# A decoder's quantised cross attention takes in the MLP behind it, pair by pair

## The chip, the cores and the metric

The program runs on one core of a Trainium2 chip. Its metric is the device time of one execution in microseconds (us). The median of three timed runs of the kernel before is 2883.2 us (2880.36 to 2885.45).

The engines are called as the profile calls them: PE is TensorE's matmuls and PEld its weight loads, DVE is VectorE, ACT is ScalarE, POOL is GpSimd, SP is SyncE, whose queue issues most DMAs here.

## What is computed

The reference is a decoder of two layers on 2048 tokens (16 tiles of 128) with 256 features. Each layer is a self attention, a cross attention and an MLP, each with a residual and a layer norm behind it. The change touches the first layer's cross attention and MLP:

```python
x = _layernorm(x + xattn(x, ctx_2048))
x = _layernorm(x + ffn(x))

# xattn: 16 heads of 16 features, 2048 queries, 2048 keys
q = fq_sym((x @ Wq + bq) * 0.25)       # 8-bit steps, one scale for a row of a head
k = fq_sym(k); v = fq_sym(v)
attn = fq_unsigned(softmax(q @ k.T))   # 0..255, one scale for a row
out  = (attn @ v) @ Wp + bp

# ffn: 1024 hidden features
h   = silu(x @ Wg.T) * (x @ Wu.T)
out = h @ Wd.T
```

## The kernel before

**Cross attention.** Keys and values are quantised first. Then a loop runs over 128 steps, `(gp, i, u)`: eight pairs `gp` of token tiles, eight pairs `i` of heads, the two tiles `u` of the pair. A step makes the scores of one tile of 128 queries for two heads against all 2048 keys.

- `scores` (L719) is called four times a step, for each half of the keys and each of the two heads. Two bf16 matmuls (L725) fill a PSUM tile `s` of two banks (three such tiles exist); DVE scales it, writes it to `e` and takes its maximum (L726). The queries stand as three copies of 16 rows in 64 rows for each head, and the key tile holds both heads in its 128 rows. For one head the other 64 rows of `qz` are zero, so a matmul runs over all 128 rows.
- `exponent` (L736): DVE reduces the four maxima to two (L738), and ACT adds ln 255 (L740).
- `weights8` (L742): ACT takes the exponential to 8 bits and its row sum (L749), and a transposing DMA on SP's queue moves it (L757).
- `spread` (L760): POOL casts the transposed bytes to bf16 (L761).
- `context` (L766): PE multiplies with the values (L771), 16 matmuls for two steps, three to four steps after the scores, in the chunks of `turns` (L810).
- `sums`, `divide`, `output` (L779 to L805) finish the pair before: reciprocals of the row sums, spread out by DVE copies (L786) and transposed by PE, the product (L796), the output projection (L802) and the residual (L805). The projection's weights `wp` are scaled by the values' scale on DVE (L697) and then laid out as `wp4` by 16 DMAs (L702).
- The queries of the next pair are made meanwhile (`query_rows`, `query_cols`, L559 and L568): a projection, and DVE instructions L542 to L549 and L563, a POOL product (L550), PE transposes (L556) and ACT copies (L572).
- The layer norm is done for four tiles at a time, `norm` (L102 to L116) and `norm_T` (L119), in every second pair: statistics, then the reciprocal root by a logarithm and an exponential on ACT (L100, L101), then a tensor_scalar on DVE (L114).

**MLP.** It begins when the cross attention has ended (L875 to L913). Both weights are loaded (3 MB). For each of four groups of 512 tokens: eight times a gate and an up product (L891), silu on ACT (L894), the product on DVE (L895); then the down product (L905), the residual (L908), and the norm of the group before.

**What sets the order.** Inside both loops the order of PE's instructions is the order of the program text (`manual_schedule`); in the MLP that holds for ACT instead. The other engines' order is made by the scheduler of the language from costs and dependences. An engine runs its instructions in that order, each waiting for its own inputs and buffers. PSUM has eight banks: six for the three `s` tiles, one for `o` of the context, one, `misc`, for everything else in the loop.

Of the kernel before, what the change touches and what calls it, by code (L numbers as in the profile page):

```python
# [18 lines left out]
F32 = mybir.dt.float32  # L19
# [29 lines left out]
def decoder(ctx: ExitStack, tc: tile.TileContext, w: dict, out: bass.AP):  # L49
# [28 lines left out]
    nc.gpsimd.memset(eps5, 1e-5)  # L78
    eps6 = const.tile([P, 1], F32, name="eps6")
# [40 lines left out]
    def norm_T(g, k, psum, tag):  # L120

        pt = psum.tile([P, 4, P], F32, tag=tag, name="ln_pt")
        for i in range(4):
            nc.tensor.transpose(pt[:, i, :], xs[4 * g + i][:, k * P : (k + 1) * P], ident)
        nc.scalar.copy(xT[g][:, k, :], pt.rearrange("p a b -> p (a b)"))

# [396 lines left out]
    with ExitStack() as ph:  # L523
# [5 lines left out]
        rows3 = [pool.tile([P, 16, 64], BF16, name=f"rows3_{i}") for i in range(2)]  # L529

        qz = [pool.tile([P, 2, 8, P], BF16, name=f"qz{i}") for i in range(4)]

        def quantised(wk, lhsT, weights, bias, scale, psum, tag):
# [3 lines left out]
            for k in range(2):  # L537
                nc.tensor.matmul(
                    pq.rearrange("p h d -> p (h d)"), lhsT=lhsT(k), rhs=weights[:, k, :], start=k == 0, stop=k == 1
                )  # L540
            a = wk.tile([P, 16, 16], F32, tag="qa", name="qa", bufs=2)
            nc.vector.tensor_tensor(a, pq, bias.rearrange("p (h d) -> p h d", h=16), ALU.add)  # L542
            s = stat.tile([P, 16], F32, tag="qs", name="qs")
            nc.vector.tensor_reduce(s, a, AX.X, ALU.max, apply_absolute_value=True)
            nc.vector.tensor_scalar(s, s, scale / 127.0, 1e-8, ALU.mult, ALU.max)
            r = stat.tile([P, 16], F32, tag="qr", name="qr")
            nc.vector.reciprocal(r, s)
            if scale != 1.0:
                nc.vector.tensor_scalar_mul(r, r, scale)  # L549
            nc.gpsimd.tensor_tensor(a, a, bc(r, 2, 16), ALU.mult)  # L550
            return a, s

        def transposed3(rows, psum, tag):
            pt = psum.tile([P, 8, P], BF16, tag=tag, name="pt3")
            for i in range(8):
                nc.tensor.transpose(pt[:, i, :], rows[:, 2 * i : 2 * i + 2, :].rearrange("p h d -> p (h d)"), ident16)  # L556
            return pt

        def query_rows(t, wk, psum, tag):  # L559

            a, s = quantised(wk, lambda k: xTt(t, k), wq, bq, 0.25, psum, tag)
            rows = rows3[t % 2]
            nc.vector.tensor_scalar(  # L563
                rows[:, :, 0:48].rearrange("p h (r d) -> p h r d", r=3), bc(a, 2, 3), ROUND, ROUND, ALU.add, ALU.subtract
            )
            return rows, s

        def query_cols(t, rows, psum, tag):  # L568
            pt = transposed3(rows, psum, tag)
            for hh in range(2):  # L570
                half = slice(64 * hh, 64 * hh + 64)
                nc.scalar.copy(qz[t % 4][half, hh], pt[half])  # L572
            return qz[t % 4]

        qs = {}
        with tc.tile_pool(name="l0x_1", bufs=1) as p1, tc.tile_pool(name="l0x_p0", bufs=2, space=PSUM) as ps0:
# [9 lines left out]
            wp = load_w(pool, "L0_xattn_Wp")  # L586
# [84 lines left out]
            for n in range(NB + 4):  # L671
# [7 lines left out]
                if n == 3:  # L679
                    for t in rows3 + qz:  # L680
                        nc.vector.memset(t, 0.0)
                if n in (5, 7):
                    t = (n - 5) // 2
                    qs[t] = query_rows(t, p1, ps0, "pk")
                if n in (6, 8):
                    t = (n - 6) // 2
                    rows, sq = qs[t]
                    qs[t] = (query_cols(t, rows, ps0, "pt3"), sq)
# [7 lines left out]
        for c in range(2):  # L696
            nc.vector.tensor_scalar(wp[:, c], wp[:, c], sv[:, c : c + 1], None, ALU.mult)  # L697
        wp4 = pool.tile([P, 4, HID], F32, name="wp4")
        nc.gpsimd.memset(wp4, 0.0)
        for h in range(16):  # L700
            at = slice(16 * (h % 8), 16 * (h % 8) + 16)
            nc.sync.dma_start(out=wp4[at, 2 * (h // 8) + h % 2, :], in_=wp[at, h // 8, :])  # L702
        ln255 = pool.tile([P, 1], F32, name="ln255")
# [10 lines left out]
        def group(gp):  # L714
            ssum = stat.tile([P, 2, 16], F32, tag="ssum", name="ssum", bufs=3)
            ot = wk.tile([P, 2, 2, 2 * P], F32, tag="ot", name="ot")
            groups[gp] = (None, ssum, ot)

        def scores(gp, i, u, half, hh, st):  # L719

            qT, sq = qs[2 * gp + u]
# [693 lines left out]
```

## Time and profile before

| what | value |
|---|---|
| median of three runs | 2883.2 us |
| the profiled execution's own time | 2880.24 us |
| its span, first to last instruction | 2878.5 us |
| mean granted TensorE clock | 0.974 |
| PE busy | 2589.4 us (90%) |
| DVE busy | 1988.7 us (69%) |
| ACT busy | 1500.2 us (52%) |
| POOL busy | 1093.5 us (38%) |
| loop of the cross attention, first to last eviction | 884.0 to 1606.0 us |
| its end: last contexts, divides, outputs, norm | 1606.0 to 1637.0 us |
| MLP, up to the next layer's first matmul | 1637.0 to 1809.6 us |

Busy shares are means over stages with different limits: PE's 90% comes from the stages around the cross attention. Inside it the shares are to be read from windows of time. Idle time of an engine that isn't the bottleneck costs nothing. A line of a group gives its source line, engine, operation, what is written and read with partitions and elements, the count, the busy time and the mean duration of one in ns, and the idle time of the engine just before these instructions with what ended it.

### The profile page before, as it was taken

The page shows a single profiled execution, that of the slowest core. Times are in us where ns is not written, and L with a number is a line of the kernel's source. Part 1 is how long each engine was busy: PE and PEld are TensorE (multiplying, and loading weights), DVE is VectorE, ACT ScalarE, POOL GpSimd, SP SyncE. Part 2 cuts the span into 40 slices and gives each one's busy share as a digit, 9 for nine tenths or more (in the row PEclk, how much of TensorE's full clock was granted, in tenths as well). Part 3 has the DMA queues.
Part 4 walks back from the last instruction along what each step waited for, and adds up shares of the span by engine and source line. Part 5 has one row for each costly group of instructions (what it writes and reads, how often), then busy time and mean ns, then how long its engine had stood idle before and what let it go on. Part 6 is the DMA issues. An engine that isn't in the chain of part 4 may idle for free.

```text
span 2878.5 us, 38462 instructions
## 1 busy us (share of the span) xinstructions
PE 2589.4 (90%) x13790; PEld 1555.3 (54%) x13868; DVE 1988.7 (69%) x4688; ACT 1500.2 (52%) x2719; POOL 1093.5 (38%) x1070
## 2 busy tenths in 40 slices
PE   6999999999976877877778699999988899999998
PEld 3677777777752333333333365566655546565646
DVE  5677877777768999999999422677877753334231
ACT  3455555555536888888888412455545432213120
POOL 4644444444465666676667400522222200000000
PEclk9999999999998999999999899999999999999999
DMA  6000000000013554554545400200010000000000
GB/s 215 1 1 1 1 1 1 1 1 1 1 52 69 93 94 85 93 98 88 91 89 96 127 12 0 96 2 1 2 52 10 3 1 0 8 1 8 0 8 8
DMA packets 298734, 108.92 MB, mean 38 GB/s; under 512 B 273328, under 2 KB 291216, under 8 KB 297776
## 3 DMA queue, kind: packets, MB, share of 16 engines
q1 hardware_dynamic: 297152, 102.65, 16.3%
q0 software_dynamic: 1392, 3.81, 0.6%
q8 instruction: 109, 1.79, 0.3%
q14 instruction: 81, 0.66, 0.1%
HBM read 36.96 MB, written 2.10 MB: 14 GB/s over the span
## 4 chain that ended last, share of the span: by engine, by line
PE 63%; DVE 20%; ACT 7%; issue 5%; POOL 2%; DMA 2%; another core or an unknown queue 0%; SPq 0%; DVEq 0%; ACTq 0%; POOLq 0%
DVE e L726 13%; PE proj L310 11%; PE gate L1322 6%; PE py L1354 6%; PE up L1322 6%; ACT a L749 4%; PE po L437 4%; PE sc L1036 3%; PE tp L1056 3%; PE o L1066 2%; PE sc L356 2%; PE pm L427 2%; PE gate L891 2%; PE pm L426 2%; PE py L905 2%
## 5 line engine op out<-in xcount | busy, mean ns | idle before, releaser
L726 DVE TENSOR_SCALAR_CACHE_REDUCE e<-s,qs 128x1024 f32<-128x1024 f32 x512 | 630.7, 1273 | 14.1 <-DMA wp<-w_L_xattn_Wp 7.7
L761 POOL CAST aT<-at 128x2048 bf16<-128x2048 uint8 x256 | 485.6, 1901 | 246.7 <-DMA at<-a 233.8
L749 ACT ACTIVATE a<-e,snl 128x2048 uint8<-128x2048 f32 x256 | 511.1, 1997 | 4.9
L725 PE MATMUL s<-kT,qz 128*128 128x512 bf16 x1001 | 309.1, 395 | 125.6 <-DVE e L726 121.5
L771 PE MATMUL o<-aT,vq 128*128 128x512 bf16 x1000 | 295.5, 399 | 26.7 <-POOL aT L761 22.1
L725 PEld LDWEIGHTS <-qz 128*128 128x128 bf16 x1024 | 101.6, 100 | 288.8 <-issue 217.9
L1326 DVE TENSOR_TENSOR h<-h,up 128x512 f32<-128x512 f32 (+1 forms) x100 | 68.8, 688 | 194.7 <-PE up L1322 193.2
L771 PEld LDWEIGHTS <-vq 128*128 128x128 bf16 x1024 | 103.2, 101 | 164.1 <-issue 50.2
L1325 ACT ACTIVATE h<-gate 128x512 f32<-128x512 f32 (+1 forms) x100 | 59.8, 598 | 238.3 <-PE gate L1322 238.1
L1322 PE MATMUL gate<-xT,w_L_ffn_w1g 128*128 128x512 f32 x352 | 167.8, 596 | 0.0
L1322 PE MATMUL up<-xT,w_L_ffn_w1u 128*128 128x512 f32 x352 | 165.4, 592 | 0.0
L1045 DVE TENSOR_REDUCE amx<-sc 128x8 f32<-128x1024 f32 x96 | 116.7, 1215 | 56.9 <-PE sc L1036 56.7
L1354 PE MATMUL py<-w_L_ffn_w2T,h 128*128 128x256 f32 x704 | 154.6, 379 | 0.0
L1048 ACT ACTIVATE pr<-pr 128x1024 f32<-128x1024 f32 x96 | 101.6, 1059 | 89.1 <-DVE pr L1047 89.0
L1057 ACT COPY prT<-tp 128x512 f32<-128x512 f32 x192 | 104.1, 584 | 76.9 <-PE tp L1056 76.6
L1354 PEld LDWEIGHTS py<-w_L_ffn_w2T,h 128*128 128x128 f32 x704 | 133.7, 190 | 18.3
L380 ACT ACTIVATE pls<-sc,lm,rms_rs 128x128 f32<-128x128 f32 x256 | 113.8, 454 | 21.7 <-DVE lm L376 21.7
L310 PE MATMUL proj<-Wlk,xT 128*128 128x512 f32 x256 | 121.9, 599 | 2.9 <-ACT raw_Wlv L336 1.7
L310 PE MATMUL proj<-Wq,xT 128*128 128x512 f32 x256 | 122.4, 601 | 0.6 <-DVE raw_Wlk L319 0.6
L437 PE MATMUL po<-Wo,mT 128*128 128x256 f32 x512 | 121.2, 380 | 1.4 <-ACT mT L429 1.4
L310 PE MATMUL proj<-Wlv,xT 128*128 128x512 f32 x256 | 121.3, 596 | 0.0
L1047 DVE TENSOR_TENSOR pr<-sc,amx 128x1024 f32<-128x1024 f32 x96 | 117.0, 1219 | 5.7
(304 smaller groups left out, 5336.2 us busy)
## 6 DMA issues: line engine op xcount, KB each, us to landing
at<-a SPq DMA_TRANSPOSE x256
w_L_ffn_w1g<-in_L_ffn_w1g SPq DMA_DIRECT2D x1, 2816.0 KB
w_L_ffn_w1u<-in_L_ffn_w1u SPq DMA_DIRECT2D x1, 2816.0 KB
w_L_ffn_w2T<-in_L_ffn_w2T SPq DMA_DIRECT2D x1, 2816.0 KB
xT<-in_xT SPq DMA_DIRECT2D x4, 512.0 KB
Wlk<-in_L_attn_Wlk SPq DMA_DIRECT2D x4, 512.0 KB
Wq<-in_L_attn_Wq SPq DMA_DIRECT2D x4, 512.0 KB
Wlv<-in_L_attn_Wlv SPq DMA_DIRECT2D x4, 512.0 KB
```

What stands on the lines that cost most here:

```text
L310: nc.tensor.matmul(pp.rearrange("p h d -> p (h d)"), lhsT=xTt(b, k), rhs=wts[nm, hg][:, k, :], start=k == 0, stop=k == 1)
L380: nc.scalar.activation(pls[:, h, :], by_head[:, h // 2, h % 2, NC4:NK], AF.Exp, bias=nm[:, h : h + 1], scale=rq[:, h : h + 1], accum_out=s ...
L437: nc.tensor.matmul(outs[b], lhsT=st["mT"][:, h, :], rhs=wts["Wo", hg][:, h, :], start=hg == 0 and h == 0, stop=hg == 3 and h == 3,)
L725: nc.tensor.matmul(s[:, c, :], lhsT=qT[:, hh, i, :], rhs=kT[:, i, at : at + G], start=True, stop=True)
L726: nc.vector.tensor_scalar(st["e"][hh][:, half, :], s.rearrange("p a b -> p (a b)"), sq[:, 2 * i + hh : 2 * i + hh + 1], None, ALU.mult, AL ...
L749: nc.scalar.activation(a.bitcast(U8), st["e"][hh].rearrange("p a b -> p (a b)"), AF.Exp, bias=st["nm"][:, hh : hh + 1], accum_out=groups[g ...
L761: nc.gpsimd.tensor_copy(aT[:, :, hh, u * P : (u + 1) * P].rearrange("p (b j) q -> p b j q", j=2), st["at"][hh].bitcast(U8).rearrange("p b ...
L771: nc.tensor.matmul(o.rearrange("p a b -> p (a b)"), lhsT=vq[:, n, c * P : (c + 1) * P], rhs=aT[:, n].rearrange("p a b -> p (a b)"), start= ...
L1045: nc.vector.tensor_reduce(mx, sc, AX.X, ALU.max)
L1047: nc.vector.tensor_tensor(pr, sc, bc(mx, 2, P), ALU.subtract)
L1322: nc.tensor.matmul(pp[:rows], lhsT=wt[:, k, :], rhs=xT[g][:, k, :], start=k == 0, stop=k == 1)
L1354: nc.tensor.matmul(py, lhsT=h[:rows, i4 * P : (i4 + 1) * P], rhs=wt, start=n == 0, stop=n == len(parts) - 1)
```

## The change

The first layer's MLP becomes part of the cross attention's loop. While pair `gp` has its scores made, pair `gp - 1` goes through its norm and its gate and up products (256 tokens at a time), and pair `gp - 2` through its down product. Only the last pair's MLP stands behind the loop. In particular:

- The MLP's gate and up weights no longer fit beside the loop's buffers. They are loaded again for each pair in 128 KB pieces, three buffers ahead of PE; for the last pair they are loaded once, into a buffer of `aT`.
- silu(g) is written as 0.5 g (1 + tanh(g/2)). ACT takes the tanh and copies gate and up out of PSUM, DVE makes (tanh + 1) g, POOL multiplies with up, and the 0.5 goes into the residual.
- The layer norms of these stages are made for pairs (`norm_pair`): the reciprocal root by a power on POOL, the subtraction and product by a scalar_tensor_tensor.
- The two heads' scores are made by matmuls over 64 rows each, one head in each row half; `qz` with its zeros becomes `qT`. The matmuls of a half-step's two `s` tiles alternate.
- The maximum of the second half starts from that of the first, and `exponent` becomes one scalar_tensor_tensor on DVE with a tile of ln 255.
- Three small steps of the query quantising, the copies of the reciprocals and the scaling of `wp4` move from DVE to POOL. The buffers of `a` go from five to four.

```diff
+    def norm_pair(q):
+        mv = stat.tile([P, 2, 2], F32, tag="np_mv", name="np_mv")
+        for i in range(2):
+            st = stat.tile([P, 6], F32, tag="ln_st", name="ln_st")
+            nc.vector.bn_stats(out=st, in_=xs[2 * q + i])
+            nc.vector.bn_aggr(out=mv[:, i, :], in_=st)
+        rstd = stat.tile([P, 2], F32, tag="np_rstd", name="np_rstd")
+        nc.gpsimd.tensor_scalar(rstd, mv[:, :, 1], 1.0, 1e-5, ALU.mult, ALU.add)
+        nc.gpsimd.tensor_tensor(rstd, rstd, mhalf, ALU.pow)
+        for i in range(2):
+            x = xs[2 * q + i]
+            nc.vector.scalar_tensor_tensor(
+                x, x, mv[:, i, 0:1], rstd[:, i : i + 1].to_broadcast([P, HID]), ALU.subtract, ALU.mult
+            )
...
         def query_rows(t, wk, psum, tag):
...
-            nc.vector.tensor_scalar(s, s, scale / 127.0, 1e-8, ALU.mult, ALU.max)
+            nc.gpsimd.tensor_scalar(s, s, 0.25 / 127.0, 1e-8, ALU.mult, ALU.max)
             r = stat.tile([P, 16], F32, tag="qr", name="qr")
             nc.vector.reciprocal(r, s)
-            if scale != 1.0:
-                nc.vector.tensor_scalar_mul(r, r, scale)
             nc.gpsimd.tensor_tensor(a, a, bc(r, 2, 16), ALU.mult)
+            nc.gpsimd.tensor_scalar(a, a, 0.25, ROUND, ALU.mult, ALU.add)
+            nc.gpsimd.tensor_scalar(
+                rows3[:, :, 0:48].rearrange("p h (r d) -> p h r d", r=3), bc(a, 2, 3), 1.0, -ROUND, ALU.mult, ALU.add
+            )
...
+        def scores(gp, i, u, half, st):
+            t = 2 * gp + u
+            s = [ps.tile([P, 2, G], F32, tag="s", name="s", bufs=3) for _ in range(2)]
             for c in range(2):
                 at = (2 * half + c) * G
+                for hh in range(2):
+                    r = slice(64 * hh, 64 * hh + 64)
+                    nc.tensor.matmul(
+                        s[hh][:, c, :], lhsT=qT[t % 4][r, i, :], rhs=kT[r, i, at : at + G], start=True, stop=True
+                    )
+            for hh in range(2):
+                nc.vector.tensor_scalar(
+                    st["e"][hh][:, half, :],
+                    s[hh].rearrange("p a b -> p (a b)"),
+                    qs[t][:, 2 * i + hh : 2 * i + hh + 1],
+                    None if half == 0 else st["mx"][:, 0, hh : hh + 1],
+                    ALU.mult,
+                    ALU.max,
+                    accum_out=st["mx"][:, half, hh : hh + 1],
+                )
 
         def exponent(st):
-            nm = stat.tile([P, 2], F32, tag="snm", name="snm")
-            nc.vector.tensor_reduce(nm, st["mx"], AX.X, ALU.max, negate=True)
             st["nm"] = stat.tile([P, 2], F32, tag="snl", name="snl")
-            nc.scalar.activation(st["nm"], nm, AF.Identity, bias=ln255)
+            nc.vector.scalar_tensor_tensor(st["nm"], st["mx"][:, 1, :], -1.0, ln255, ALU.mult, ALU.add)
...
+        def ffn_load(j):
+            i, n = j // 2, j % 2
+            t = wgu[i, n] = wk.tile([P, 2, P], F32, tag="wgu", name="wgu", bufs=3)
+            nc.sync.dma_start(out=t, in_=gu_dram[n, i])
...
+        def ffn_gate(q, i, n, tag="misc"):
+            if n == 0:
+                pp = ps.tile([P, 2, G] if tag == "s" else [P, 2, 2 * P], F32, tag=tag, name="gu", bufs=3 if tag == "s" else 1)
+                ffn_ps[q] = pp[:, 0].rearrange("p (n c) -> p n c", n=2) if tag == "s" else pp
+            at = slice((q % 2) * 2 * P, (q % 2) * 2 * P + 2 * P)
+            wt = wgu[i, n]
+            for k in range(2):
+                nc.tensor.matmul(
+                    ffn_ps[q][:, n, :], lhsT=wt[:, k, :], rhs=xT[q // 2][:, k, at], start=k == 0, stop=k == 1
+                )
+
+        def ffn_mult(q, i, tail=False):
...
+            nc.scalar.activation(th, pp[:, 0], AF.Tanh, scale=0.5)
+            nc.scalar.copy(gu, pp)
+            nc.vector.scalar_tensor_tensor(th, th, 1.0, gu[:, 0], ALU.add, ALU.mult)
+            (nc.vector if tail and i % 2 else nc.gpsimd).tensor_tensor(hs[q][:, i], th, gu[:, 1], ALU.mult)
+
+        def ffn_down(q, u, c, tag="misc"):
...
+            for i in range(NI):
+                nc.tensor.matmul(
+                    pd, lhsT=hs[q][:, i, u * P : (u + 1) * P], rhs=wd[:, i, at], start=i == 0, stop=i == NI - 1
+                )
+            x = xs[2 * q + u][:, at]
+            nc.vector.scalar_tensor_tensor(x, pd, 0.5, x, ALU.mult, ALU.add)
...
+        def pair_work(n, end):
+            gp, r = n // 16, n % 16
+            if 0 < gp <= NB // 2:
+                if (r, end) in ((4, 1), (5, 0)):
+                    divide(gp - 1, r - 4)
+                elif (r, end) in ((5, 1), (6, 0)):
+                    output(gp - 1, r - 5)
+                    if r == 6:
+                        norm_pair(gp - 1)
+                elif (r, end) == (7, 1):
+                    norm_pair_T(gp - 1, ps, "misc")
+            if gp + 1 < NB // 2:
+                if (r, end) in ((0, 1), (3, 1)):
+                    qs[2 * gp + 2 + r // 3] = query_rows(2 * gp + 2 + r // 3, wk, ps, "misc")
+                elif (r, end) in ((2, 1), (7, 0)):
+                    query_cols(2 * gp + 2 + r // 7, ps, "misc")
+            if 0 < gp < NB // 2:
+                q = gp - 1
+                j = 2 * (r - 8) + end
+                if -3 <= j < 0:
+                    ffn_load(j + 3)
+                if r >= 8:
+                    ffn_gate(q, r - 8, int(end))
+                    if end:
+                        ffn_mult(q, r - 8)
+                    if j + 3 < 2 * NI:
+                        ffn_load(j + 3)
+            if gp > 1 and not end and r < 4 and gp - 2 < NB // 2 - 1:
+                ffn_down(gp - 2, r // 2, r % 2)
+                if r == 3:
+                    norm_pair(gp - 2)
+            if gp > 1 and end and r == 6 and gp - 2 < NB // 2 - 1:
+                norm_pair_T(gp - 2, ps, "misc")
```

`pair_work` is called at the end of each half-step; the separate MLP stage (L875 to L913) is removed, and behind the loop the last pair's gate, up and down products follow with the `s` tiles as their PSUM.

## The prediction

> **What bounds the kernel now.** I read the page's lines first, then a table of windows cut at the first eviction of each pair of token tiles, then the timeline. In the page's lines the last parts are busy us, mean ns of one, and idle time before with its cause. POOL is GpSimd, DVE VectorE.
>
> ```profile
> L726 DVE TENSOR_SCALAR_CACHE_REDUCE e<-s,qs 128x1024 f32<-128x1024 f32 x512 | 630.7, 1273 | 14.1 <-DMA wp<-w_L_xattn_Wp 7.7
> L761 POOL CAST aT<-at 128x2048 bf16<-128x2048 uint8 x256 | 485.6, 1901 | 246.7 <-DMA at<-a 233.8
> L749 ACT ACTIVATE a<-e,snl 128x2048 uint8<-128x2048 f32 x256 | 511.1, 1997 | 4.9
> ```
>
> The windows (start and end, length, then busy us and counts of PE, PE's weight loads, DVE, ACT and POOL, granted clock, DMA share, GB/s):
>
> ```profile
> 1153.20:1241.90 88.70, 70.05 (x295) 30.93 (x300) 87.30 (x166) 77.86 (x92) 61.69 (x34) 0.98 0.53 95
> 1241.90:1337.70 95.80, 73.75 (x301) 33.10 (x308) 94.55 (x176) 80.26 (x98) 62.09 (x35) 0.93 0.46 88
> ...
> 1606.00:1637.00 31.00, 17.10 (x60) 8.39 (x59) 7.15 (x24) 8.74 (x13) 13.96 (x27) 0.82 0.35 99
> 1637.00:1809.60 172.60, 170.33 (x536) 100.47 (x536) 42.91 (x93) 31.85 (x50) 5.68 (x18) 0.98 0.10 27
> ```
>
> The cross attention runs from 884.0 to 1606.0 us, eight pairs, 722 us, and **DVE sets it**: 87.3 of 88.7 us busy in a pair without layer norm, 94.6 of 95.8 in one with it. Evictions (L726) wait for no more than 14.1 us in all. The drain takes 31 us; then the MLP takes 172.6 us with TensorE busy for 170.3 and DVE for 43. The change lays the second stage into the first, whose own bound has no room: all turns on what it does to DVE.
>
> The second thing to see is how long a DVE instruction takes while POOL works:
>
> ```profile
> 1201.62 3.86 POOL L761 CAST aT<-at 128x2048 bf16<-128x2048 uint8 x2 [0.62 <-DMA at<-a]
> ...
> 1203.84 1.67 DVE L545 TENSOR_SCALAR qs<-qs 128x16 f32<-128x16 f32 x1
> ...
> 401.00 0.41 DVE L230 TENSOR_TENSOR raw_Wq<-rope_a,rope_b 128x256 f32<-128x256 f32 x1
> ...
> 407.86 1.04 POOL L408 TENSOR_TENSOR pls<-pls,sums 128x512 f32<-128x512 f32 x1
> ...
> 408.16 1.03 DVE L230 TENSOR_TENSOR raw_Wlk<-rope_a,rope_b 128x256 f32<-128x256 f32 x1
> ```
>
> L545 on sixteen columns takes 0.16 us with POOL idle and 1.67 here: it ends when the cast ends. L230, which reads two SBUF tensors, takes 0.41 alone and 1.03 when it meets a POOL instruction. Even a 128x4 one (L376) goes from 0.137 to 0.52. Instruction by instruction, duration is the lone one plus what is left of POOL's, less 0.13 us. Evictions (PSUM in, 1.27) never show it.
>
> **What the skill says.** The Trainium skill, "SBUF — State Buffer", section "SBUF: two separate sides": VectorE and GpSimd share a port pair under an exclusive lock, which a VectorE instruction takes in a two-port mode or with two SBUF inputs; the other blocks for the whole instruction. The numbers above agree. "TensorEngine Tiling (Array Packing)", "Key Properties": row tiles compute in parallel, a change of tiling mode drains the array. The trace agrees on the first: four f32 passes of 512 columns take 1.06 us as two 64-row blocks (L1036, 2202.21 to 2203.27) and 1.72 with 128 rows (L891, 1790.39 to 1792.11). "ScalarE: Activation LUTs", "Table sets: the hidden batching unit": exp and tanh lie in one set, so tanh costs one load, not one per use; a load is 1283 ns in this trace.
>
> **The change, part by part.** Time unit: a pair (16 steps of four evictions).
>
> *Base.* Undisturbed steps come every 4.88 us (from one L738 to the next, five in a row after 890, and the most frequent distance later): 4 x 1.20 plus 0.07 for L738. 16 x 4.88 = 78.1. Check on the pair of 88.7: queries 2 x (0.418+0.412+0.80+0.243+0.68+1.67) = 8.4, sums and copies 1.0, divides 2 x 0.68, outputs 2 x 0.41; less 0.07 overlap for each of 16 instructions: 88.6. The method holds.
>
> *Query quantising.* Three DVE instructions per tile go to POOL; the other three stay: 2 x 1.07 = 2.1. That removes 6.3 us per pair, mostly lock waits. The L786 copies also go (0.6). The reciprocal now waits for a POOL instruction that can queue behind a cast (0 to 1.9 us); evictions are behind it. In the trace other evictions were put in such gaps, so I take nothing here and keep up to 3 us a pair for the range.
>
> *Sums, divides, outputs* stay: 2.5. *Attention norm*, now for every pair: statistics 2 x (0.40+0.16), two scalar_tensor_tensor of 0.48 (L1240's shape): 2.1. *MLP norm*: 2.1 more. *MLP product*, eight of 0.48: 3.9. *Down sums*, four 128x128 with PSUM in: 0.29 each (L1078), 1.2. Base and these: 92.0; less 0.07 for 30 overlaps: **90**.
>
> *Locks.* The new scalar_tensor_tensor all read two SBUF tensors: 16 exponents (L738 before was one-input and free), 8 products, 4 norms. For the exponents I took, at every L738 start from 900 to 1600 us, what was left of POOL's instruction, less 0.13: mean 0.36. Two-port rows of today wait 0.52 (L549), 0.64 (L545), 0.80 (L114), 1.1 (L563). I take 0.36, 0.6 and 0.8: 5.8+4.8+3.2 = **13.8**. Bounds: 0 (POOL always idle then; a gain is excluded, a wait can't be negative) and 28 x 0.95 = 27 (half a cast each time).
>
> *POOL.* Now 62 us a pair. Added: queries 2 x (0.35+0.63+about 1.0; the 768-wide one lies between 0.71 by the cast's rate and 1.8 by L550's), copies 1.0, eight products of 0.63, norm scalars about 1.4 (no row shows a power; even 2 us each is hidden by POOL's idle time, except for the norm behind it). About 73 of 106: its busy share stays at 70%, so lock waits keep their rate.
>
> *ACT.* Removed: L740, 16 x 0.29; half of the L572 copies, 2.0. Added: eight times 0.37 (tanh) and 0.59 (copy), one transposed copy. About 82 us per pair: off the path while steps exceed 5.6.
>
> *TensorE.* Scores in halves: a pair of tiles takes about 0.65 us instead of 0.86 with a drain. Gate and up: 64 passes of 256 columns at 0.216 (L905: 64 in 13.81) = 13.8. Down: 64 passes of 128 columns at 0.11 (L426, L427) = 7.0. In an MLP step: 1.3 scores, 1.7 context, 1.7 gates, 4.7 of 6. Hidden. But both score tiles of a half-step are now written together out of three buffers, so TensorE has room for about 2.3 us of other work there before DVE starves. Gates plus context: 2.15. Down plus context: 1.76+1.07 = 2.8 twice a pair. With the one "misc" bank, which passes from user to user each half-step, I take 2 us a pair (0 to 8).
>
> *SP.* 16 weight loads a pair, issue about 0.45 each (L87), stand between transposes; each waits for a gate's matmul that is under way by then. 2 MB a pair adds 20 GB/s to 93. If transposes land later, casts start later; POOL's idle time covers that. Projection weights for wp4 come straight from DRAM: the 7.7 us at the first eviction was in truth TensorE's wait for a PSUM release (L621), so nothing is gained.
>
> *Sum.* Pair 0: 78.1+2.1+5.8 = 86. Pairs 1 to 6: 90+13.8+2 = 106. Pair 7, without queries: 104. Total 826, against 722: **+104**. The drain keeps its 31. The MLP's 172.6 become a tail of one pair: gates 13.8 plus 2.7 for a cold clock, last product 2, down 7: 25.5; **-147**. The next layer's first weights land during the down products; in the trace they needed none of the path. Net -43. The profiled execution took 2880.2 (span 2878.5 and 1.7 around it), 3 us under the median: 2880.2 - 43 = 2837.
>
> **Rivals.**
>
> *A. Locks mostly miss.* For it: at L738 POOL is idle half of the time. Pair 0 at 83, the others at 97, the last at 95: 760, +38 - 147: **2771**. Chance 0.20.
>
> *B. Slower: the exponent pins the step to its own cast.* From exponent to the cast of the same step the trace gives 0.25 to the activation, 2.0, then 3.2: the cast holds the lock from 5.45 to 7.35 us. An exponent that comes after 5.45 waits until 7.2. Plain steps (4.9) escape; steps with MLP or norm work (5.5 to 7.2 of their own) all become 7.2. 13 x 7.2 + 3 x 4.9 + 2 x 2.3 for the second cast in the two norm steps = 113, with 2 for TensorE 115: 86 + 6 x 115 + 113 = 889, +167 - 147: **2900**. It decides from a pair of 112 on (86+7x112-2 = 868 = 722+147). Against it: ACT busy with the tanh, or a late transpose, moves the cast. Chance 0.28.
>
> *C. The gain is eaten exactly.* The single "misc" bank stalls the scores: 21 uses a pair, 0.3 us each, on top of my sum gives 112, **2880**. Against it: evictions wait 14 us in all today. Chance 0.07.
>
> *D. The halves don't run side by side* (each matmul drains). 0.2 to 0.35 us more per half-step push the gate slots over TensorE's room; about 4 us per pair: 2837+28 = **2865**. L1036 speaks against it. Chance 0.03.
>
> **How the numbers follow.** My forecast has 0.42, and its own spread (locks 9 to 18 a pair) is 2805 to 2868. Faster: 0.42+0.20+0.03 = 0.65; within 0.2% (about what a measurement of this kernel can tell from no change): C, 0.07; slower: B, 0.28. The range goes from a pair of 95 (2757) to one of 117 (2914), leaving out the outer parts of A and B.
>
> **What would show it.** Right: the MLP's window gone, a tail near 25 us, pairs of 103 to 109 with DVE over 95% busy, exponents far longer than 0.15 us on average. Step B: exponents that end with a cast's end, steps of 7.2 us. A: exponents at 0.15 and pairs under 98. C: evictions waiting for TensorE, TensorE for "misc" readers. It would be wrong if the two-input exponent didn't take the lock against a one-input cast (only TENSOR_SCALAR is seen against casts), or if another engine had steps of its own over 6 us.

## The result, and the profile after

The changed kernel takes **2909.9 us** (median of four, 2906.4 to 2916.2) against 2883.8 for the kernel before in the same session: ratio **1.0095**, 95% interval 1.0074 to 1.0115. It is slower, where I forecast 2837. Its profiled execution took 2906.4 us, with a span of 2904.4.

Groups of the page, busy us, mean ns of one, idle before and what ended it:

```profile
L760 ACT ACTIVATE a<-e,snl 128x2048 uint8<-128x2048 f32 x256 | 510.7, 1997 | 219.6 <-issue 127.7
L772 POOL CAST aT<-at 128x2048 bf16<-128x2048 uint8 x256 | 487.8, 1911 | 245.4 <-DMA at<-a 234.8
L739 DVE TENSOR_SCALAR_CACHE_REDUCE e<-s,qs,smx 128x1024 f32<-128x1024 f32 x256 | 332.4, 1330 | 17.5 <-PE s L735 17.4
L739 DVE TENSOR_SCALAR_CACHE_REDUCE e<-s,qs 128x1024 f32<-128x1024 f32 x256 | 324.6, 1275 | 18.6 <-PE s L735 18.0
```

The evictions are now two forms, and the one with a pointer as its initial value is 55 ns longer; both wait for TensorE, 35 us in all instead of 14. ScalarE and GpSimd do their main work in the time of before. Pairs 0, 2, 4 and 7, and the tail, in windows (columns as in the table of before):

```profile
889.90:980.80 90.90, 67.56 (x244) 19.23 (x247) 86.52 (x148) 65.65 (x67) 57.00 (x36) 0.76 0.45 84
...
1088.00:1205.90 117.90, 91.38 (x428) 44.66 (x436) 107.12 (x183) 79.76 (x94) 73.26 (x55) 0.90 0.48 90
...
1319.00:1429.00 110.00, 88.18 (x427) 42.91 (x435) 102.47 (x181) 79.27 (x92) 73.23 (x56) 0.94 0.52 96
...
1657.30:1771.10 113.80, 84.35 (x395) 39.65 (x403) 106.09 (x172) 77.06 (x90) 68.07 (x47) 0.91 0.48 89
1771.10:1802.00 30.90, 22.75 (x120) 15.65 (x120) 9.18 (x25) 6.41 (x8) 9.77 (x11) 0.89 0.31 87
1802.00:1828.30 26.30, 23.14 (x128) 20.66 (x128) 7.52 (x22) 8.16 (x17) 5.22 (x12) 0.94 0.06 19
```

The last row is the whole of what is left of the MLP stage: 26.3 us. The pairs are what went wrong: pair 0 is 91, pairs 1 to 7 are 107 to 118, mean 112.9, and VectorE is idle for 7.5 to 11 us in each of the later ones shown. Against the two profiled executions:

| stretch | before | after | difference |
|---|---|---|---|
| to the first eviction | 884.0 | 889.9 | +5.9 |
| eight pairs | 722.0 | 881.2 | +159.2 (forecast +104) |
| drain and MLP, to the same point in the next layer's start | | | -143.7 (forecast -147) |
| rest | | | +4.5 |

The +4.5 arises around 2200 us, far inside the next layer. A kernel below that has nothing of the change behind the loop (f1_form) shows it too, and two that have all of it there (e2_norm, h1_halfpasses) do not, so it isn't the change's; it is called stray below. It goes with the granted TensorE clock: 0.92 from 2180 to 2225 us here, 1.00 in the same part of the kernel before (2159 to 2200). Why the clock differs there stays open; comparisons of e2 and h1 with the changed kernel contain this difference. The +5.9 comes in the keys' preparation, between 820 and 870 us. f2_offload below has the same moves of the query quantising to GpSimd and starts its loop at 886.0 us, 2.0 later than the kernel before; the rest of the +5.9 was not split further.

The instructions with two inputs in SBUF are the exponent (L751, from the maxima to the activation's bias), the product (L860, (tanh + 1) g) and the norm (L141). A lock is the time that such an instruction stands still while GpSimd works. Their groups in pairs 1 to 7 (980.8 to 1771.1 us):

```profile
L751 DVE SCALAR_TENSOR_TENSOR snl<-smx,ln 128x2 f32<-128x2 f32 x112 | 54.7, 488 | 1.0
L860 DVE SCALAR_TENSOR_TENSOR th<-th,gu_s 128x256 f32<-128x256 f32 x55 | 48.9, 889 | 1.2 <-ACT gu_s L859 0.7
L141 DVE SCALAR_TENSOR_TENSOR x<-x,np_mv,np_rstd 128x256 f32<-128x256 f32 x26 | 39.1, 1543 | 11.5 <-POOL np_rstd L138 11.5
```

Undisturbed they take 0.15, 0.42 and 0.48. So locks cost 112 x 0.338 + 55 x 0.469 + 26 x 1.063 = 91 us, 13.0 a pair; I had 13.8. What VectorE waits for while idle, in the same stretch (us in total, times, longest):

```profile
DVE e L739 <- PE s L735: 24.6, 18, 2.4
DVE x L141 <- POOL np_rstd L138: 11.5, 8, 2.7
DVE x L873 <- PE pd L869: 10.4, 11, 2.6
DVE qa L567 <- PE pq L563: 6.3, 5, 1.8
DVE qr L572 <- POOL qs L570: 2.5, 2, 1.9
```

With smaller ones that is 60 us, 8.6 a pair, where I had 2. The longest of these waits, 2.41, is the same in each of the seven pairs. This is the one of pair 4: the gate's first matmuls and the scores behind them, then the next of both (TensorE, with the eviction):

```profile
1378.51 2.07 PE L844 MATMUL gu<-xT,wgu 128*128 128x256 f32 x4 [2.03 <-ACT xT L151]
1380.51 1.04 PE L735 MATMUL s<-kT,qT 64*128 64x512 bf16 x4
...
1381.58 1.34 DVE L739 TENSOR_SCALAR_CACHE_REDUCE e<-s,qs,smx 128x1024 f32<-128x1024 f32 x1 [2.41 <-PE s L735]
...
1383.09 1.03 PE L844 MATMUL gu<-xT,wgu 128*128 128x256 f32 x4
...
1384.05 0.61 PE L735 MATMUL s<-kT,qT 64*128 64x512 bf16 x4
```

Two things make it. The gate waits for ScalarE's copy of the normalised rows, the user of the `misc` bank before it. Then gate and scores take 3.1 us where the next ones take 1.6: the granted TensorE clock is 0.50 from 1378.5 to 1381.6 us, and 1.00 from 1382.8 to 1387.3. From these four rows I estimate the clock's part at 1.5 of the 2.41 us. All seven gates take 2.07 here, and 17.6 of the 24.6 us before evictions lie in stretches at half clock.

And here is one step of the loop in which a lock is paid, in the timeline of the changed kernel (start, duration, engine, line; TensorE, the queue of SP and the evictions left out):

```profile
1390.68 0.41 DVE L751 SCALAR_TENSOR_TENSOR snl<-smx,ln 128x2 f32<-128x2 f32 x1
...
1391.12 2.00 ACT L760 ACTIVATE a<-e,snl 128x2048 uint8<-128x2048 f32 x1 [0.59 <-DVE snl L751]
...
1393.12 1.99 ACT L760 ACTIVATE a<-e,snl 128x2048 uint8<-128x2048 f32 x1
...
1396.01 0.58 ACT L859 COPY gu_s<-gu 128x512 f32<-128x512 f32 x1
1396.37 1.89 POOL L772 CAST aT<-at 128x2048 bf16<-128x2048 uint8 x1 [0.68 <-DMA at<-a]
1396.84 1.70 DVE L860 SCALAR_TENSOR_TENSOR th<-th,gu_s 128x256 f32<-128x256 f32 x1
1398.46 0.15 DVE L751 SCALAR_TENSOR_TENSOR snl<-smx,ln 128x2 f32<-128x2 f32 x1
```

The exponent (L751) ends at 1391.09. It releases two activations; their first result, transposed, starts a cast (L772) 5.28 us later. In the same time VectorE does four evictions and the product before, and comes to the next product 5.75 us after the exponent: 0.47 us into the cast that this very exponent set off. It could not have come much before: ScalarE copies the gate (L859) behind both activations and is done 5.50 us after the exponent. That product ends 0.28 us after the cast, 7.45 us after the exponent, and the next exponent, behind it, finishes 7.52 after the last. **A ring:** exponent, activation, transpose, cast, lock, exponent. Of the 42 exponents of pairs 1 to 7 that took over 0.35 us, 25 ended with the first cast of the step just before; that cast comes 5.42 us after its exponent (median, 5.27 at least). Of the 111 steps of pairs 1 to 7, from one exponent's end to the next one's, 35 took 7.2 to 7.6 us.

### The profile page after: what moved, and what is told of

Read it like the earlier page. It is cut to its first block, busy times and chain, and to the rows that moved or that the text cites. A ratio compares the mean times of both kernels' runs of the same rounds, so it can differ in the third digit from the quotient of the medians.

```text
span 2904.4 us, 40170 instructions
## 1 busy us (share of the span) xinstructions
PE 2581.7 (89%) x14288; PEld 1556.1 (54%) x14380; DVE 2046.1 (70%) x4669; ACT 1469.6 (51%) x2650; POOL 1183.0 (41%) x1229
## 5 line engine op out<-in xcount | busy, mean ns | idle before, releaser
L772 POOL CAST aT<-at 128x2048 bf16<-128x2048 uint8 x256 | 487.8, 1911 | 245.4 <-DMA at<-a 234.8
L739 DVE TENSOR_SCALAR_CACHE_REDUCE e<-s,qs,smx 128x1024 f32<-128x1024 f32 x256 | 332.4, 1330 | 17.5 <-PE s L735 17.4
L739 DVE TENSOR_SCALAR_CACHE_REDUCE e<-s,qs 128x1024 f32<-128x1024 f32 x256 | 324.6, 1275 | 18.6 <-PE s L735 18.0
L735 PE MATMUL s<-kT,qT 64*128 64x512 bf16 x1024 | 215.7, 415 | 106.5 <-DVE e L739 104.5
L782 PE MATMUL o<-aT,vq 128*128 128x512 bf16 x963 | 276.3, 416 | 6.6 <-issue 4.4
L782 PEld LDWEIGHTS <-vq 128*128 128x128 bf16 x1024 | 90.8, 103 | 183.4 <-issue 115.8
L844 PE MATMUL gu<-xT,wgu 128*128 128x256 f32 x448 | 126.2, 406 | 42.1 <-ACT gu_s L859 27.1
L735 PEld LDWEIGHTS <-qT 64*128 64x128 bf16 x1024 | 41.1, 95 | 226.0 <-issue 220.3
L844 PEld LDWEIGHTS gu<-xT,wgu 128*128 128x128 f32 x448 | 86.8, 200 | 79.8 <-ACT gu_s L859 40.7
```

What stands on the lines that cost most here:

```text
L735: nc.tensor.matmul(s[hh][:, c, :], lhsT=qT[t % 4][r, i, :], rhs=kT[r, i, at : at + G], start=True, stop=True)
L739: nc.vector.tensor_scalar(st["e"][hh][:, half, :], s[hh].rearrange("p a b -> p (a b)"), qs[t][:, 2 * i + hh : 2 * i + hh + 1], None if hal ...
L772: nc.gpsimd.tensor_copy(aT[:, :, hh, u * P : (u + 1) * P].rearrange("p (b j) q -> p b j q", j=2), st["at"][hh].bitcast(U8).rearrange("p b ...
L782: nc.tensor.matmul(o.rearrange("p a b -> p (a b)"), lhsT=vq[:, n, c * P : (c + 1) * P], rhs=aT[:, n].rearrange("p a b -> p (a b)"), start= ...
L844: nc.tensor.matmul(ffn_ps[q][:, n, :], lhsT=wt[:, k, :], rhs=xT[q // 2][:, k, at], start=k == 0, stop=k == 1)
```

## The experiments

Theory after the result: VectorE sets the pair, and the locks, the eviction's form and the waits that I mis-sized add up. Rivals: TensorE and its one bank bound the pair, so that locks only hide; two inputs are not the cause of the locks. First each lock by itself, then all three. Each time is given as a ratio to the kernel before on the same chip.

**e1_exponent.**

```diff
-nc.vector.scalar_tensor_tensor(st["nm"], st["mx"][:, 1, :], -1.0, ln255, ALU.mult, ALU.add)
+nc.vector.tensor_reduce(st["nm"], st["mx"][:, :, 1:3], AX.X, ALU.add, negate=True)
```

(`mx`, which the evictions write, becomes one of four fixed tiles 128x2x3, whose last column holds -ln 255.)

> Of the changed kernel only the exponent is altered: one reduction (VectorE, one SBUF input) over the maximum and a constant column in place of the scalar_tensor_tensor with two SBUF inputs. Theory (VectorE bounds the pair, locks are paid in full): the instruction takes about 0.15 us each time instead of 0.44 to 0.49 on average, and the 44 us that the exponents wait in pairs 1 to 7, and 4.5 in pair 0, go: about 2862 (2855 to 2870). Rival 1 (TensorE and its one misc bank bound the pair): the saved waits come back as idle time before evictions, less than 15 us gained, above 2890. Rival 2 (the lock has nothing to do with two inputs): the exponent still averages above 0.35 us, no gain.

2884.5 us, ratio 1.0009 (1.0003 to 1.0016): 25 us under the changed kernel (from the ratios), half of what the theory said. The groups in its pairs 1 to 7:

```profile
L861 DVE SCALAR_TENSOR_TENSOR th<-th,gu_s 128x256 f32<-128x256 f32 x55 | 61.2, 1112 | 1.2 <-ACT gu_s L860 1.2
L141 DVE SCALAR_TENSOR_TENSOR x<-x,np_mv,np_rstd 128x256 f32<-128x256 f32 x26 | 39.1, 1543 | 13.3 <-POOL np_rstd L138 13.3
...
L752 DVE TENSOR_REDUCE snl<-smx 128x2 f32<-128x4 f32 x112 | 16.7, 149 | 1.0
```

The exponent is free of the lock: the same two columns, one input instead of two, and never over 0.161 us. The operation changed with the inputs; e3 below has the same operation with one input fewer in SBUF, and is free as well. But the product, unchanged, went from 0.889 to 1.112: a third of what the exponents lost came back there. VectorE's idle time rose too, from 60 to 69 us. VectorE's instructions have the same order as in the changed kernel, all 873 in the loop.

**e2_norm.**

```diff
-nc.vector.scalar_tensor_tensor(
-    x, x, mv[:, i, 0:1], rstd[:, i : i + 1].to_broadcast([P, HID]), ALU.subtract, ALU.mult
-)
+nc.gpsimd.tensor_scalar(x, x, mv[:, i, 0:1], rstd[:, i : i + 1], ALU.subtract, ALU.mult)
```

> Of the changed kernel only the normalisation itself moves: (x - mean) * rstd is computed by GpSimd, right behind its own power, instead of VectorE's scalar_tensor_tensor with two SBUF inputs. Theory (VectorE bounds): its 28 instructions of 1.54 us in the loop go (40 us) and the 11.5 us that it waits for the power: about 2862 (2855 to 2872); GpSimd gets some 0.4 to 0.6 us more for each, which its idle time hides. Rival 1 (TensorE and the misc bank bound): under 20 us gained. Rival 3 (GpSimd is now late for the transposes of the normalised rows): the gain is under 20 us and TensorE waits for GpSimd.

2892.0, ratio 1.0037 (1.0025 to 1.0050): 17 us gained, a third of the theory's.

```profile
L749 DVE SCALAR_TENSOR_TENSOR snl<-smx,ln 128x2 f32<-128x2 f32 x112 | 74.5, 665 | 1.0
```

VectorE lost 40 us of work and 11.5 of waiting; exponents rose from 0.488 to 0.665, products from 0.889 to 0.967 (24 us in all), and the reciprocal waits 10.3 us for GpSimd instead of 2.5, the outputs' sums 6.8 for TensorE instead of next to none. In its trace the loop is 19 us shorter than in the changed kernel, what stands behind it, with its own norm now on GpSimd, is 7 longer, and the stray 4.5 is missing.

**e3_product.**

```diff
-nc.scalar.copy(gu, pp)
-nc.vector.scalar_tensor_tensor(th, th, 1.0, gu[:, 0], ALU.add, ALU.mult)
+nc.scalar.copy(gu[:, 1], pp[:, 1])
+nc.vector.scalar_tensor_tensor(th, th, 1.0, pp[:, 0], ALU.add, ALU.mult)
```

> Of the changed kernel only the first MLP product is altered: VectorE reads the gate from PSUM, so that it has one SBUF input; ScalarE copies only the up half. Theory (two SBUF inputs take the lock, PSUM doesn't): the instruction falls from 0.89 us to about 0.45 and 25 us go: about 2885 (2878 to 2893). Rival 1 (the misc bank bounds): the bank is now held until VectorE comes to the product, behind its evictions; evictions wait longer for TensorE and the time is the same or longer, 2905 to 2930.

2942.5, ratio 1.0213 (1.0198 to 1.0228): **34 us slower** than the changed kernel, in the rival's direction by more than it said. Evictions wait 21 us for TensorE, less than in the changed kernel (25). The groups:

```profile
L751 DVE SCALAR_TENSOR_TENSOR snl<-smx,ln 128x2 f32<-128x2 f32 x112 | 93.0, 830 | 0.5
...
L860 DVE SCALAR_TENSOR_TENSOR th<-th,gu 128x256 f32<-128x256 f32 x55 | 23.1, 419 | 34.8 <-ACT gu_s L859 34.7
```

The product is free of the lock (0.419, 26 us less) and the exponent took the wait over: 0.488 to 0.830, 38 us more. A second loss is nearly as large: VectorE stands idle for 35 us before the products, until ScalarE's copy is done, where it had 1. A step of it:

```profile
1409.20 0.92 DVE L751 SCALAR_TENSOR_TENSOR snl<-smx,ln 128x2 f32<-128x2 f32 x1
...
1415.61 0.42 DVE L860 SCALAR_TENSOR_TENSOR th<-th,gu 128x256 f32<-128x256 f32 x1 [0.55 <-ACT gu_s L859]
1415.95 1.50 DVE L751 SCALAR_TENSOR_TENSOR snl<-smx,ln 128x2 f32<-128x2 f32 x1
```

The cast runs from 1415.55 to 1417.44 (5.43 us after the exponent above). The product passes through it; the exponent behind it stops until its end. Half of the gate steps (25 of 49) are 7.2 to 7.6 us.

This edit also moved something: VectorE's order in the loop isn't written by hand, the compiler places it. Read from the traces over seven gate steps of one pair (e eviction, P product, X exponent):

```
changed kernel, e1, e2: X ePeeeX ePeeePX eeeeeX PeeeeX PeeeeX PeeeX ePeeeX
e3, e4, e8:             X PeeeeX PeeeePX eeeePX eeeePX eeeePX eeeePX eeeePX
```

So, in these three kinds, e1 and e2 are clean against the changed kernel, and e3, e8 and e4 against each other. e3 is not clean against the changed kernel. With P right ahead of X the exponent comes behind ScalarE's copy, which itself comes behind both activations of the exponent before: in the step above the copy ends 5.4 us after that exponent, where the cast begins. How much of e3's 34 us is the freed product and how much the order isn't separated.

**e4_three**: the edits of e1, e2 and e3 together.

> The three edits together (exponent by one input, normalisation on GpSimd, product with the gate from PSUM). Theory: the sum of the three, some 110 to 125 us less than the changed kernel, 2785 to 2800, which is also under the kernel before. Rival 1 (TensorE and the misc bank bound): pairs stay above 105 us, evictions wait over 10 us a pair, above 2845.

**2811.4, ratio 0.9768** (0.9748 to 0.9789): 94 us under the changed kernel, where the three alone sum to -8, and 67 under the kernel before (from the ratios). One of its pairs, and its groups:

```profile
1172.30:1271.20 98.90, 84.04 (x428) 42.22 (x436) 90.51 (x176) 77.95 (x92) 76.83 (x59) 0.97 0.53 107
```

```profile
L859 DVE SCALAR_TENSOR_TENSOR th<-th,gu 128x256 f32<-128x256 f32 x55 | 23.1, 421 | 11.7 <-ACT gu_s L858 11.3
...
L750 DVE TENSOR_REDUCE snl<-smx 128x2 f32<-128x4 f32 x112 | 16.8, 150 | 0.5
```

Of the 49 gate steps (the last seven of each of pairs 1 to 7) none is at 7.2 to 7.6 now; they average 5.81 us, against 6.44 in the changed kernel and 7.24 in e3. Pairs are 99, so the rival (over 105) falls. VectorE is still idle for 8.7 us a pair, as in the changed kernel (8.6): what is gained in pairs 1 to 7, 99 us, is about what the three instructions held VectorE for in addition (38, 26 and, with the norm's own work, 40). So the gain is the locks'. TensorE's clock was granted more of the time too (half clock for 8% of pairs 1 to 7, against 18%), but VectorE's idle time is no shorter for it.

**e8_expprod**: e4_three with the norm left on VectorE, against the sum of single effects.

> The changed kernel with two of the three edits of e4_three: exponent by one input and product with the gate from PSUM; the normalisation stays on VectorE. Theory (a ring: the product and the exponent behind it come 5.3 to 6 us after the exponent before, the first cast of that step 5.42 us after it, and whichever of the two takes the lock waits until the cast's end near 7.3): freeing both opens the ring though each alone did not, so the steps with gates fall from 6.4 us towards 5.8 and the time to 2845 to 2865, with the norms' 40 us still to pay. Rival (the edits' effects add up as they were measured singly, -25 and +33): 2910 to 2920.

2840.6, ratio 0.9860 (0.9843 to 0.9876). The single effects don't add. At one and the same order of VectorE (all 873 instructions of the loop), e3 to e8 (exponent freed) is **-102 us**; at the changed kernel's order the same edit gave -25. In pairs 1 to 7 the exponents lose 76 us of it, and VectorE's wait before the products falls from 35 us to 14. With the exponent alone in the ring (e3) 25 of 49 gate steps take 7.2 to 7.6 us; with the product alone (e1) 7 do, but they still average 6.33; with neither, none does, and they average 5.86. e8 to e4, the norm, is -27.

**f1_form** and **f2_offload**: two parts of the change alone, on the kernel before.

```diff
 sq[:, 2 * i + hh : 2 * i + hh + 1],
-None,
+None if half == 0 else st["mx"][:, hh, 0:1],
```

> The kernel before, with one thing of the change: the second half's eviction takes the first half's maximum as its initial value (a pointer in place of None). The reduction that follows stays. Theory ([...]1.330 against 1.275 us in the trace of the changed kernel): 256 evictions on VectorE's path by 0.055 to 0.07 us: 14 to 18 us slower, about 2897. Rival (the 0.055 us overlaps with the evictions' fill): 2882, no change.

2902.0, ratio 1.0067 (1.0052 to 1.0082): +19 us. In the trace an eviction of the new form takes 1333 ns against 1275, and the instruction behind it starts 1.266 us after it instead of 1.204; 256 x 0.062 is 16 us. The loop is 19 us longer there, the compiler's order of some small instructions changed as well, and the stray 4.8 around 2200 us is in it, so the 19 us can't be given to the form alone:

```profile
L726 DVE TENSOR_SCALAR_CACHE_REDUCE e<-s,qs,smx 128x1024 f32<-128x1024 f32 x256 | 333.9, 1333 | 0.2
L726 DVE TENSOR_SCALAR_CACHE_REDUCE e<-s,qs 128x1024 f32<-128x1024 f32 x256 | 323.9, 1275 | 17.1 <-DMA wp<-w_L_xattn_Wp 7.7 <-ACT a L749 6.3 <-PE s L725 1.9
```

f2, per tile:

```diff
-nc.vector.tensor_scalar(s, s, scale / 127.0, 1e-8, ALU.mult, ALU.max)
+nc.gpsimd.tensor_scalar(s, s, scale / 127.0, 1e-8, ALU.mult, ALU.max)
...
-nc.vector.tensor_scalar(
-    rows[:, :, 0:48].rearrange("p h (r d) -> p h r d", r=3), bc(a, 2, 3), ROUND, ROUND, ALU.add, ALU.subtract
-)
+nc.gpsimd.tensor_scalar(a, a, 0.25, ROUND, ALU.mult, ALU.add)
+nc.gpsimd.tensor_scalar(
+    rows[:, :, 0:48].rearrange("p h (r d) -> p h r d", r=3), bc(a, 2, 3), 1.0, -ROUND, ALU.mult, ALU.add
+)
```

> The kernel before, with one thing of the change: three of the query quantising's VectorE instructions per tile go to GpSimd. Theory (as in my sum: 6.3 us of VectorE a pair go, less what the reciprocal now waits for GpSimd, 0 to 3 us a pair): seven pairs by 3.3 to 6.3, less some 6 us before the loop: 2842 to 2865. Rival (the reciprocal waits a full cast each time, in front of the evictions): within 0.3% of the kernel before.

2866.0, ratio 0.9941 (0.9924 to 0.9957), just above the theory's range: -17. In the loop it takes the 38 us of three VectorE instructions away and 16 us of new idle time come (6.7 for the reciprocal behind GpSimd, the rest before evictions).

**h1_halfpasses.**

```diff
-for k in range(2):
+for k in range(2 if tag == "s" else 1):
...
-for i in range(NI):
+for i in range(last + 1):
```

> The changed kernel with half of TensorE's MLP passes inside the loop left out (one of two gate passes, four of eight down passes; so the MLP's values are not those of the reference); all waits, copies and VectorE instructions stay. It takes some 10 us of TensorE out of each of seven pairs. If VectorE starves because TensorE has too little room between evictions, its waits for TensorE (42 us in pairs 1 to 7) fall to under half, and the time by 20 us or more, to 2885 or less. If it starves because the single misc bank and the th and gu buffers pass from user to user (ScalarE's and GpSimd's queues), little changes: 2895 to 2910.

2893.3, ratio 1.0038 (1.0025 to 1.0051), between the two. VectorE's idle time before evictions grew to 36 us (28 of it ended by TensorE, 8 by ScalarE's copy), that before the queries' sum is 5, that for the downs is gone: 41 in all, as in the changed kernel. But TensorE did not get the room that was meant: it ran at half clock for 27% of pairs 1 to 7 instead of 18%, and 24 of the 36 us lie there. The compiler's order changed as well (PeeeeX in nearly every gate step), and 4.5 of the 17 us are the stray ones. So this run decides nothing between passes and bank.

**k2_early_after** and **k1_early**: another edit at the same question, on the changed kernel and on e4_three.

```diff
-if (r, end) in ((4, 1), (5, 0)):
-    divide(gp - 1, r - 4)
-elif (r, end) in ((5, 1), (6, 0)):
-    output(gp - 1, r - 5)
-    if r == 6:
+if r == 4:
+    divide(gp - 1, end)
+elif r == 5:
+    output(gp - 1, end)
+    if end:
         norm_pair(gp - 1)
-elif (r, end) == (7, 1):
+elif (r, end) == (7, 0):
...
-elif (r, end) in ((2, 1), (7, 0)):
+elif (r, end) in ((2, 1), (7, 1)):
```

> The changed kernel with the attention's divides, outputs and norm of each pair half a step to a step earlier, and the transposes of the normalised rows half a step earlier, so that the MLP's first gate finds them copied. In the changed kernel an eviction waits 2.41 us in each of seven pairs for scores that are queued behind this gate. Theory (these waits of TensorE for a reader through the misc bank are the larger part of the idle time that my 2 us a pair missed): seven times 2.4 us go, about 2893 (2885 to 2899). Rival (another wait, of the locks, takes their place): within 6 us of 2910.

> e4_three with the same edit. There evictions wait 0.88 and 0.63 us a pair in this place, and the downs and outputs 1.6: theory, 7 to 15 us under e4_three, 2796 to 2804. Rival (the query's columns, half a step later now, are late instead): no gain or a loss of some us.

k2: 2897.6, ratio 1.0063 (1.0042 to 1.0085), some 9 us under the changed kernel; the two intervals overlap, so the gain isn't shown, and the trace has it elsewhere than expected. The place of the 2.41 us in k2:

```profile
1381.64 2.07 PE L844 MATMUL gu<-xT,wgu 128*128 128x256 f32 x4 [2.88 <-ACT qT L584]
...
1384.72 1.34 DVE L739 TENSOR_SCALAR_CACHE_REDUCE e<-s,qs,smx 128x1024 f32<-128x1024 f32 x1 [2.84 <-PE s L735]
```

The gate waited for ScalarE's copy of the rows; now it waits for ScalarE's copy of the query's columns, the bank's user before it, which sits behind an activation in the same way. It runs at half clock again (2.07), and the eviction's wait is 2.84 instead of 2.41. The norms gain: in pairs 1 to 7 they wait 4.5 us for the power instead of 11.5 and take 0.80 us instead of 1.54, 19 us less; but the exponents rise from 0.488 to 0.583, 11 us more. k1: 2832.0 (0.9832), 18 us slower than e4; VectorE's idle time in pairs 1 to 7 is 82 us instead of 61, before evictions, products and reciprocals. So the wait isn't this transpose's alone. It does go away in two places. In pair 7 of k2, which makes no queries, that gate takes 1.13 us and the eviction waits 0.11. In e4 that gate takes 1.13 in five of seven pairs, and no eviction beside it waits over 0.89 us; in the two pairs where it takes 2.07 and 2.08, evictions beside it wait up to 1.60 and 3.32. Waiting reader and half clock come together there, and no run parts them.

**e5_oldform, e6_late, e7_two**: three attempts to go below e4. e5 has the evictions and the exponent of before (no initial value, ln 255 added on ScalarE); e6 is e4 with the query's reciprocal half a step later; e7 is e6 without the initial value and with two reductions, as shown here.

```diff
-nc.vector.tensor_reduce(st["nm"], st["mx"][:, :, 1:3], AX.X, ALU.add, negate=True)
+nc.vector.tensor_reduce(st["snm"][:, :, 0], st["mx"], AX.X, ALU.max, negate=True)
+nc.vector.tensor_reduce(st["nm"], st["snm"], AX.X, ALU.add)
```

> As e4_three (normalisation on GpSimd, product with the gate from PSUM), with the exponent and the evictions of the kernel before: no initial value, one reduction over both maxima on VectorE, ln 255 added on ScalarE. Theory: the exponent is as free of locks, and 256 evictions lose 0.055 us each: 14 us under e4_three's 2811, about 2797, less some 2 us for the longer chain. Rival: the 0.3 us that the chain from maximum to cast gets longer and ScalarE's extra instruction cost as much: 2811.

> e4_three with the query's reciprocal issued one half-step later, so that VectorE has evictions to do while GpSimd scales (behind its casts). The reciprocal's 16.7 us of idle time in pairs 1 to 7 go: theory 2793 to 2800. Rival (ScalarE or TensorE is next, and the wait only moves): 2806 to 2812.

> e6_late without the initial value: both halves' maxima, then two small reductions on VectorE (maximum, then the sum with a constant column), each with one SBUF input. 256 evictions lose 0.06 to 0.074 us each, 128 exponents gain 0.07 to 0.15: 6 to 12 us under e6_late. Rival (ScalarE paces the gate steps, so that VectorE's time there is free): within 4 us of e6_late.

2851.9 (0.9889), 2822.4 (0.9798) and 2847.7 (0.9890): all slower than e4. In e5 and e7 evictions are back at 1.274 and 1.276 us, but VectorE is idle for 114 and 95 us in pairs 1 to 7 instead of 61, before evictions and down sums; the order that the compiler gave the products differs again (in e7 some gate steps hold three evictions and others five). In e6 the reciprocal still waits twelve times, 18 us: it did not move behind other work (VectorE's order in the loop is that of e4). So the form's 0.06 us could not be had back here, and why VectorE starves in e5 and e7 was not taken further.

## Why the prediction was wrong

**Right.** VectorE as the busiest engine of a pair, though it is busy for 92% of pairs 1 to 7 and not for over 95%. The MLP's tail: 26.3 us measured against 25.5, and drain and MLP together -143.7 against -147. The locks' size, 13.0 us a pair against 13.8, exponents 5.4 against 5.8, products 3.7 against 4.8, norms 3.9 against 3.2. The sum without locks: e4 has no norm arithmetic on VectorE (4 x 0.48) and the new form (32 x 0.062, the 1.266 us instead of 1.204 above), so it should be 90 - 1.9 + 2.0 = 90.1; it is 90.5. That the halves of TensorE run side by side: four 512-column matmuls in 0.60 us. That tanh costs one table load: the loop has one (L858, 1283 ns) for 56 of them. That ScalarE's and SP's additions lie off the path holds for their busy time.

**The step that failed: the pair's sum, 106 (105.7 as a mean of pairs 1 to 7), which is 112.9.** Two terms of it:

- VectorE's idle time: *"I take 2 us a pair (0 to 8)"* for TensorE, and *"so I take nothing here"* for GpSimd. VectorE is idle 8.6 us a pair: 3.5 before evictions, 1.5 before down sums, 0.9 before the query's sum, and 2.0 for GpSimd (0.4 of it the reciprocal; 1.6 the norm behind the power, which queues behind a cast: named in the prediction, but not in its sum). I had reasoned on how much TensorE has to do, at full clock. In the longest waits the gate stands for the bank's reader, a ScalarE copy behind an activation, with the scores queued behind it, and then gate and scores run at half clock (2.07 and 1.04 us). TensorE is at half clock for 143 of the 790 us of pairs 1 to 7; the sum has a cold clock in the tail alone. Whether the bank alone, with a full clock, would cost more than my 2 us stays open, as h1 and k2 left both in place. Rival C named the bank, at 21 x 0.3 = 6.3 us a pair on top of my sum; the waits for TensorE are 5.9 in all, with the clock's part in them, and stand beside other misses.
- *The evictions at 1.20 us in the base.* The change gives every second one a pointer as its initial value, and I priced it at nothing. f1 has 0.062 us for each, 2.0 us a pair.

90 + 2.0 + 13.0 + 8.6 = 113.6, against 112.9. Pair 0 likewise: 90.9 against 86, with 2.0 for the form and 4.3 of idle time. The loop is 55 us over my sum; these two terms, 6.6 + 2.0 less 0.8 of locks in seven pairs, give 55, and with pair 0's 4.9 it is 60, 5 too many. The kernel crossed the point that rival B gave, 112 a pair.

**Right in size for the wrong reason: the locks.** I added them as independent accidents, from where the old exponent met GpSimd. In the steps with gates they hang together in a ring. e1, e2 and e3 changed the time by -25, -17 and +34, and all three by -94 (e3's and e4's include another order of VectorE). A part of a lock that is taken away at one instruction is paid at another that needs it: a third of it in e1, 24 us for the norm's 28 in e2, 38 us for the product's 26 in e3. Rival B had the mechanism, *"the exponent pins the step to its own cast"*, with 7.2 us a step; steps of 7.2 to 7.6 exist, but 35 of 111, not 91; why not more are held was not taken apart. Its 2900 came near for a part of its reason.

The Trainium skill, "SBUF — State Buffer", section "SBUF: two separate sides", says that the loser of the lock blocks for the whole instruction. The runs agree, down to the smallest case: two columns with two SBUF inputs took up to 1.88 us, with one SBUF input never over 0.161 (e1), and the product with one input from PSUM 0.42 while casts ran.

## What to carry to other kernels

Before an edit adds a two-SBUF-input VectorE instruction to a loop in which GpSimd works in long pieces, follow what that instruction releases: if it starts, some engines later, the GpSimd piece that the next such instruction meets, the step can lock to that period. A lock's gain can't be read off one instruction: here freeing the exponent gave 25 us while the product still took the lock, and 102 when the product was free and stood elsewhere in the order. Look at every engine's order before comparing two versions, since an edit of one instruction moved others. And when work is to go through one PSUM bank, price the reader's queue, and read the granted clock where TensorE goes on behind the wait.

## What was not expected of the hardware

- An eviction with a pointer as the initial value of its maximum takes 1330 to 1337 ns (means of the runs) against 1275 with none (128x1024, PSUM in), and comes every 1.27 us instead of 1.20.
- The power of two columns on GpSimd takes 0.71 us (L138), its scaling 0.19: cheap, but both queue behind casts of 1.9, and the norm that they release takes 1.54 on average instead of 0.48.
- TensorE's clock was at half for 18% of pairs 1 to 7 in the changed kernel, 27% with half of the MLP's passes left out (h1), 8% in e4 and 10% in the kernel before: less work for TensorE did not bring more clock.
